# A selective scan whose products are shared by VectorE and GpSimd: which tiles GpSimd takes, when a pair of tiles is summed, and how much background work each step may start

## The chip, the cores and the metric

The kernel runs on one core of one Trainium2 chip. The metric is the device time of one execution in microseconds (us). TensorE (PE) multiplies matrices, VectorE (DVE), ScalarE (ACT) and GpSimd (POOL) compute on tiles, and SyncE (SP) issues nearly all transfers. All data are 32-bit floats.

## The reference, cut to what matters

Eight images of 64 x 64 positions and 96 channels go through two layers. The first is a state-space layer: a projection to 192 channels, a 3 x 3 convolution per channel, and then, along each of four directions over the 4,096 positions, a recurrence for every one of the 192 channels and 16 states.

```python
def step(h, inp):
    ul, dl, Bl, Cl = inp
    dA = jnp.exp(dl[..., None] * A)
    h = dA * h + (dl * ul)[..., None] * Bl[:, :, None, :]
    y = jnp.einsum('bkdn,bkn->bkd', h, Cl)
    return (h, y)
```

The four results are added, normalised, gated and projected back. The second layer doubles the resolution, applies a two-layer network with a quadratic activation and filters down again. Each layer's output is added to its input.

## The kernel before, in words

**The foreground: one tile per step.** A tile is 128 partitions (8 channels x 16 states) by 1,024 positions. 24 tiles (`NT`) cover the 192 channels of one chunk of 1,024 positions, four chunks (`NCH`) make a direction, and four directions (`k`, in the order 1, 0, 2, 3) make an image: 384 tiles an image, 3,072 in all. A loop takes one tile per step, so a step is the unit of everything below, and 96 steps (one direction) are called a quarter. A tile passes through these operations:

- `fetch` (L1001), six steps ahead: a transfer puts du (the product of dl and u) into `dub`, each channel's row repeated for its 16 states. Behind it, `product_b` (L1007) on GpSimd, three steps ahead: `bb = dub * br`.
- `decay` (L1013 and L1020), one step ahead: TensorE spreads dl over the states into the PSUM tile `pd`, and ScalarE takes the exponential in place. `pd` has two buffers, so the decay of tile p+1 has to wait until tile p-1 has left its buffer.
- `scan` (L1027) on VectorE: the recurrence. For most tiles its result overwrites `pd`. For a tile with the mark `by_pool` it goes to an SBUF tile `h`.
- `product_c` (L1033): `hc = h * cr`. VectorE does it straight after the scan. For a `by_pool` tile GpSimd does it in the next step, ahead of that step's `product_b`. These are called pooled tiles here.
- `hold` (L1037): the scan's last column is kept for the next chunk, by VectorE, or by ScalarE for a pooled tile.
- `sums` (L1056, and L1068, which adds what earlier directions left): TensorE adds the 16 states, for two tiles at a time, into `py`. Then ScalarE copies `py` out (L1089) and it is stored. `hc` has four buffers.

So an unpooled tile leaves its `pd` after scan, product and hold. A pooled tile leaves it right after the scan.

**The order.** Each engine works its instructions in the order in which the loop issues them. In one step this is: the pooled product of tile i-1, `product_b` of tile i+3, the decay of tile i+1, scan, product and hold of tile i, then background work, then (in every second step) the sums of a pair.

**The background.** All other work of both layers is written as generators that are advanced once per step: the preparation of the next chunk (px L924, pv L949, dl L965, u L968), convolution and gates of the next image (L515 to L581), normalisation of the last one (ty, pm, po, L637 to L706) and its second layer (L749 to L873). Each piece states an estimated cost per engine. `advance` adds an allowance per step to what is left for each engine, up to a limit, and takes off the cost of what it starts; a piece that does not fit waits for a later step:

```python
CAPS = dict(pe=(2.1, 2.9), act=(2.3, 3.0), dve=(1.5, 1.5), pool=(1.4, 2.7))
self.left = {e: min(self.left.get(e, 0.0) + c, most) for e, (c, most) in caps.items()}
self.left["pe"] -= taken
```

`taken` is 0.95 for a step with sums, and as much again where L1068 runs. Independent of this, a pace for the whole image decides how many pieces may be under way. Before the loop there is a preparation of about 140 us, and after the last step the second layer of the last image is run out with no allowance.

Of the kernel before, what the change touches and what calls it, by code (L numbers as in the profile page):

```python
# [25 lines left out]
NT = DI // 8  # L26
# [11 lines left out]
class Side:  # L38
# [6 lines left out]

    CAPS = dict(pe=(2.1, 2.9), act=(2.3, 3.0), dve=(1.5, 1.5), pool=(1.4, 2.7))

    def __init__(self, pool):
        self.pool = pool
# [79 lines left out]
def kernel(ctx: ExitStack, tc: tile.TileContext, a: dict, out: bass.AP):  # L132
# [78 lines left out]
    with tc.tile_pool(name="ps0", bufs=1, space=PSUM) as ps0, tc.tile_pool(name="setup", bufs=1) as c0p:  # L211
# [41 lines left out]
        for quarter in range(2):  # L253
            for n in (SIDE, 64):
                at = cols[n, quarter] = slice(c0, c0 + n)
# [96 lines left out]
    side = Side(pss)  # L352
# [625 lines left out]
    tiles = []  # L978
    for b in range(images):
        for k in (1, 0, 2, 3):  # L980
            order = range(NCH) if k < 2 else range(NCH - 1, -1, -1)
            for n, c in enumerate(order):
                got = {}
                for i in range(NT):
                    q, n8 = divmod(i, 8)
                    s, j = n8 % 2, n8 // 2
                    tiles.append(
                        dict(b=b, k=k, i0=c * T, first=n == 0, i=i, q=q, s=s, j=j, g=8 * q + 4 * s + j, got=got)
                    )

                    beside = b > 0 if k == 1 else k == 3 and b == images - 1
                    tiles[-1]["by_pool"] = i % (4 if beside else 3) == 2
    carry = pp.tile([128, NT], F32, tag="carry", name="carry", bufs=1)

    summed = set()
# [1 line left out]
    def fetch(t):  # L997
        assert t["got"]["ready"]
        t["dub"] = sp.tile([128, T], F32, tag="dub", name="dub", bufs=4)
        g = t["g"]  # L1000
        nc.sync.dma_start(  # L1001
            t["dub"], t["got"]["du"][None, 8 * g : 8 * g + 8, :].to_broadcast([NS, 8, T])
        )

    def product_b(t):
        t["bb"] = sp.tile([128, T], F32, tag="bb", name="bb", bufs=4)
        nc.gpsimd.tensor_tensor(t["bb"], t["dub"], t["got"]["br"], ALU.mult)  # L1007

    def decay(t):
        pd = t["pd"] = psd.tile([128, T], F32, tag="pd", name="pd")  # L1010
        for hf in range(2):
            rows = slice(64 * hf, 64 * hf + 64)
            nc.tensor.matmul(  # L1013
                pd[:, MB * hf : MB * hf + MB],
                sel_b[rows, 4 * t["s"] + t["j"]].rearrange("p n c -> p (n c)"),
                t["got"]["dl"][rows, t["q"], :],
                start=True,
                stop=True,
            )
        nc.scalar.activation(pd, pd, AF.Exp, scale=neg_a[:, t["k"], t["g"] : t["g"] + 1])  # L1020
# [10 lines left out]
    def product_c(t):  # L1031
        t["hc"] = sp.tile([128, T], F32, tag="hc", name="hc", bufs=4)
        (nc.gpsimd if t["by_pool"] else nc.vector).tensor_tensor(t["hc"], t["h"], t["got"]["cr"], ALU.mult)  # L1033
# [7 lines left out]
    def parts(t):  # L1041

        o = y_dram[t["b"]][t["k"] % 2]
        q = t["q"]
        return [o[64 * q : 64 * q + 64, t["i0"] + MB * hf : t["i0"] + MB * hf + MB] for hf in range(2)]

    def sums(two):

        t0 = two[0]
        if t0["j"] == 0:  # L1050
            t0["got"]["py"] = psy.tile([128, MB], F32, tag="py", name="py")
        py = t0["got"]["py"]
        for t in two:
            for hf in range(2):
                r0 = 64 * hf + 32 * t["s"]
                nc.tensor.matmul(  # L1056
                    py[r0 : r0 + 32],
                    sel_r[:, t["j"], :],
                    t["hc"][:, MB * hf : MB * hf + MB],
                    start=(t["j"] == 0),  # L1060
                    stop=(t["j"] == 3 and t["k"] == 0),
                    skip_group_check=True,
                )

        if t0["j"] == 3 and t0["k"]:

            add = d_diag[:, t0["q"], :] if t0["k"] == 1 else ident
            nc.tensor.matmul(py, add, t0["got"]["yp"], start=False, stop=True, skip_group_check=True)  # L1068
# [17 lines left out]
    def store(t):  # L1086
        yield dict(act=0.7)
        yq = sp.tile([128, MB], F32, tag="yq", name="yq", bufs=1)
        nc.scalar.copy(yq, t["got"]["py"])  # L1089
        yield {}  # L1090
        for hf, part in enumerate(parts(t)):
            nc.sync.dma_start(part, yq[64 * hf : 64 * hf + 64])
        if t["q"] == Q3 - 1:
            if t["k"] == 3:
                summed.add((t["b"], t["i0"] // T))
            elif t["k"] == 2 and t["i0"] == 0:
                summed.add((t["b"], "even"))
# [3 lines left out]
    with tc.manual_schedule():  # L1101
        side.queue, rest = front(0)
        side.drain()
        side.urgent = prepare(0, tiles[0]["k"], tiles[0]["i0"], tiles[0]["got"])
        side.drain()
        n = len(tiles)
        for i in range(FETCH):
            fetch(tiles[i])
            if i >= FETCH - LEAD:
                product_b(tiles[i - FETCH + LEAD])  # L1110
        decay(tiles[0])
        begin, *side.later = prepare(0, tiles[NT]["k"], tiles[NT]["i0"], tiles[NT]["got"])
        side.urgent.append(begin)
        total = 1
        for i in range(n + 4):
            t = tiles[i] if i < n else None
            at = i % (NT * NCH * K)
            if t and t["i"] == 0:
                b = t["b"]
                if at == 0:  # L1120
                    y_dram[b] = [dr.tile([DI, L], F32, tag=f"y{o}", name=f"y{o}") for o in range(2)]
                    side.begun, hasty = 0, sum(item[1] for item in rest) if b == 0 else 0
                    side.queue += rest
                    down, end = [], []
                    if b:
                        keep = {}
                        side.queue += tail(b - 1, keep)
                        up, down, end = mlp(b - 1, keep)
                        side.queue += up
                    if b + 1 < images:  # L1130
                        start, rest = front(b + 1)
                        side.queue += start[:2] + [i for two in zip(down, start[2:10]) for i in two] if b else start[:10]
                        side.queue += start[10:] + rest
                        rest = []
                    else:
                        side.queue += down
                    side.queue += end
                    total = sum(item[1] for item in side.queue)
                if b == images - 1 and at == NT * NCH * (K - 1):
                    keep = {}  # L1140
                    side.queue += tail(b, keep, pairs=False)
                    total = 0

            if i % NT == 20 and i + 4 + NT < n:
                nxt = tiles[i + 4 + NT]
                begin, *side.later = prepare(nxt["b"], nxt["k"], nxt["i0"], nxt["got"])
                side.urgent.append(begin)
            if i % NT == 0:
                side.urgent += side.later
                side.later = []  # L1150
            if t and t["i"] % 8 == 4:
                before(t)
            if i + FETCH < n:
                fetch(tiles[i + FETCH])
            if 0 < i <= n and tiles[i - 1]["by_pool"]:
                product_c(tiles[i - 1])
            if i + LEAD < n:
                product_b(tiles[i + LEAD])
            if i + 1 < n:
                decay(tiles[i + 1])  # L1160
            if t:
                scan(t)
                if not t["by_pool"]:
                    product_c(t)
                hold(t)
            ends = i % 2 == 1 and 3 <= i <= n + 2
            adds = ends and tiles[i - 2]["j"] == 3 and tiles[i - 2]["k"]
            side.advance(
                Side.CAPS,
                2 if not total or side.begun < max(hasty, total * at / 290) else 0,  # L1170
                0 if 7 <= i % NT <= 21 else 1,
                0.95 * (bool(ends) + bool(adds)),
            )
            if ends:
                sums(tiles[i - 3 : i - 1])
                if tiles[i - 2]["j"] == 3:
                    side.stores.append([g := store(tiles[i - 2]), next(g)])
        up, down, end = mlp(images - 1, keep)
        side.queue += up + down + end
        side.drain()  # L1180
# [89 lines left out]
```

## Time and profile before

| | |
|---|---|
| time, median of 3 runs | 11,521.71 us (11,514.94 to 11,524.55) |
| the profiled execution | 11,526.07 us, span 11,524.0 us |
| busy in the span | DVE 10,419.6 us, POOL 10,195.9 us, PE 9,523.4 us, ACT 5,877.0 us |
| mean granted TensorE clock | 0.913 |
| transfers | 2,401 MB, mean 208 GB/s |
| first scan starts, last sums start | 143.7 us, 11,241 us |

A scan takes VectorE about 2.3 us and a product 1.2 us; the same product takes GpSimd 2.36 us. The matmuls of one decay are four records in the trace and take about 1.1 us together. The profile's chain of what ended last holds only the run-out after the last scan, so the stretch that matters, the 3,072 steps, has to be read from the groups, the waits and the timeline. A wait that depends on several semaphores is named after the one that came last, so the engine named is not always the one that was late.

### The profile page before, as it was taken

The numbers are of one execution on the slowest core, as the hardware profiler recorded it, in microseconds if no ns is written. First come the engines' busy times: TensorE is split into PE (matmuls) and PEld (weight loads), VectorE is DVE, ScalarE is ACT, GpSimd is POOL, SyncE is SP. The second block draws the span as 40 slices with busy tenths as digits, with TensorE's granted clock in tenths as the row PEclk, the third lists the DMA queues.
The fourth block names the chain that finished last, engine by engine and source line by source line (L and its number), as shares of the span: only waits on it lengthen the run. The fifth ranks groups of instructions, "written<-read, shape, count | busy, mean of one in ns | idle before, by whom it ended". The sixth has DMA issues, their size and how long they took to land. (4 is left out here: it accounts for less than half of the span.)

```text
span 11524.0 us, 133552 instructions
## 1 busy us (share of the span) xinstructions
PE 9523.4 (83%) x42840; PEld 3036.7 (26%) x42840; DVE 10419.6 (90%) x8549; ACT 5877.0 (51%) x8210; POOL 10195.9 (88%) x4729
## 2 busy tenths in 40 slices
PE   7787768988789887888779897798977989788878
PEld 2121112322123222332223321232212322123225
DVE  5999999999999999999999999999999999899990
ACT  4455444556455454555545555454554546445443
POOL 4899998989989899999999998998999989899980
PEclk8898888999899998999889998899989999889987
DMA  6888898889988898898988889888898889988971
GB/s 150 205 196 221 201 217 202 209 217 233 221 201 212 214 229 217 207 215 216 235 204 215 213 210 240 201 213 212 218 234 205 214 212 232 218 200 211 230 189 47
DMA packets 1045088, 2401.01 MB, mean 208 GB/s; under 512 B 293948, under 2 KB 315708, under 8 KB 1044392
## 3 DMA queue, kind: packets, MB, share of 16 engines
q1 hardware_dynamic: 1040872, 2391.03, 84.3%
q8 instruction: 345, 5.65, 0.2%
q14 instruction: 351, 2.88, 0.1%
q10 hardware_dynamic: 3520, 1.46, 0.1%
HBM read 1929.05 MB, written 328.73 MB: 196 GB/s over the span
## 5 line engine op out<-in xcount | busy, mean ns | idle before, releaser
L1007 POOL TENSOR_TENSOR bb<-dub,br 128x1024 f32<-128x1024 f32 x3072 | 7174.9, 2358 | 357.9 <-DVE pd L1027 175.2
L1020 ACT ACTIVATE pd<-pd,neg_a 128x1024 f32<-128x1024 f32 x3072 | 3338.8, 1087 | 4952.4 <-PE pd L1013 4682.4
L1013 PE MATMUL pd<-dl,sel_b 64*128 64x512 f32 x12288 | 3833.8, 696 | 1781.3 <-DVE carry L1037 1556.1
L1027 DVE TENSOR_TENSOR_SCAN pd<-pd,carry,bb 128x1024 f32<-128x1024 f32 x1584 | 3722.4, 2350 | 328.0 <-ACT carry L1037 243.5
L1033 POOL TENSOR_TENSOR hc<-h,cr 128x1024 f32<-128x1024 f32 x960 | 2262.9, 2357 | 565.0 <-DVE h L1027 456.1
L1033 DVE TENSOR_TENSOR hc<-pd,cr 128x1024 f32<-128x1024 f32 x2112 | 2586.4, 1225 | 182.3 <-PE py L1056 43.5
L1013 PEld LDWEIGHTS pd<-dl,sel_b 64*128 64x128 f32 x12288 | 1053.2, 199 | 4243.7 <-issue 2837.3
L1056 PE MATMUL py<-hc,sel_r 128*32 128x512 f32 x12288 | 1839.2, 674 | 16.2 <-ACT yq L1089 15.5
L1027 DVE TENSOR_TENSOR_SCAN h<-pd,carry,bb 128x1024 f32<-128x1024 f32 x720 | 1684.3, 2339 | 51.6 <-ACT pd L1020 51.1
L1027 DVE TENSOR_TENSOR_SCAN pd<-pd,bb 128x1024 f32<-128x1024 f32 x528 | 1209.9, 2292 | 159.6 <-ACT carry L1037 129.8
L515 PE MATMUL pc<-pad,convr 96*128 96x512 f32 (+1 forms) x2304 | 867.9, 618 | 1.7 <-issue 1.7
L968 POOL TENSOR_TENSOR u<-dl,u 128x512 f32<-128x512 f32 x384 | 485.4, 1272 | 127.9 <-DMA br<-xd 127.8
L1027 DVE TENSOR_TENSOR_SCAN h<-pd,bb 128x1024 f32<-128x1024 f32 x240 | 547.4, 2281 | 17.3 <-ACT pd L1020 16.6
L1056 PEld LDWEIGHTS py<-hc,sel_r 128*32 128x32 f32 x12288 | 252.7, 113 | 1151.2 <-issue 838.8
L802 PEld LDWEIGHTS p<-w2q,mq 128*100 128x100 f32 x4800 | 454.5, 169 | 275.4 <-issue 212.4
L924 PE MATMUL px<-u,xp 64*64 64x512 f32 x1536 | 455.8, 650 | 78.6 <-DMA u<-u 78.6
L795 PE MATMUL ph<-xu,w 96*128 96x500 f32 x960 | 509.6, 635 | 10.9 <-ACT mq L796 6.1
L802 PE MATMUL p<-w2q,mq 128*100 128x96 f32 x4800 | 513.2, 259 | 2.7 <-ACT mq L796 2.7
L949 PE MATMUL pv<-xd,dt_w 64*64 64x512 f32 x1536 | 412.1, 629 | 9.4 <-ACT xd L934 9.2
L515 PEld LDWEIGHTS pc<-pad,convr 96*128 96x128 f32 (+1 forms) x2304 | 264.1, 163 | 570.2 <-issue 564.1
L796 ACT ACTIVATE mq<-ph,b 128x500 f32<-128x500 f32 x480 | 322.1, 678 | 73.2 <-PE ph L795 71.1
L1037 DVE COPY carry<-pd 128x1 f32<-128x1 f32 x2112 | 311.7, 148 | 0.0
(142 smaller groups left out, 6259.1 us busy)
## 6 DMA issues: line engine op xcount, KB each, us to landing
dub<-du SPq DMA_DIRECT2D x3072, 512.0 KB
u<-u SPq DMA_DIRECT2D x256, 384.0 KB
du<-u SPq DMA_DIRECT2D x768, 128.0 KB
y<-yq SPq DMA_DIRECT2D x768, 128.0 KB
br<-xd SPq DMA_DIRECT2D x256, 256.0 KB
cr<-xd SPq DMA_DIRECT2D x256, 256.0 KB
yp<-y SPq DMA_DIRECT2D x384, 128.0 KB
yp<-u SPq DMA_DIRECT2D x192, 128.0 KB
```

Of the source, the lines that this page charges most:

```text
L515: nc.tensor.matmul(t[rows].rearrange("p (i j) -> p i j", i=8), weights[:, cs], v["pad"][:, 8 * blk + kw : 8 * blk + kw + 8, kh : kh + H], ...
L795: nc.tensor.matmul(t[:, :px], w1[:, m, :], xu, start=True, stop=True)
L802: nc.tensor.matmul(t[:SIDE, C * i : C * i + C], sq[:, m, row], w2q[:, m, :], start=(m == 0), stop=(m == 2))
L924: nc.tensor.matmul(p[rows], xp[rows, k, q, :], v["u"][rows, q, :], start=(q == 0), stop=(q == 2), skip_group_check=True,)
L949: nc.tensor.matmul(t[rows], dt_w[rows, k, 64 * q : 64 * q + 64], v["xd"][rows], start=True, stop=True, skip_group_check=True,)
L968: nc.gpsimd.tensor_tensor(v["u"][:, q, :], got["dl"][:, q, :], v["u"][:, q, :], ALU.mult)
L1007: nc.gpsimd.tensor_tensor(t["bb"], t["dub"], t["got"]["br"], ALU.mult)
L1013: nc.tensor.matmul(pd[:, MB * hf : MB * hf + MB], sel_b[rows, 4 * t["s"] + t["j"]].rearrange("p n c -> p (n c)"), t["got"]["dl"][rows, t[" ...
L1020: nc.scalar.activation(pd, pd, AF.Exp, scale=neg_a[:, t["k"], t["g"] : t["g"] + 1])
L1027: nc.vector.tensor_tensor_scan(t["h"][:, ::step], pd[:, ::step], t["bb"][:, ::step], 0.0 if t["first"] else held, ALU.mult, ALU.add)
L1033: (nc.gpsimd if t["by_pool"] else nc.vector).tensor_tensor(t["hc"], t["h"], t["got"]["cr"], ALU.mult)
L1056: nc.tensor.matmul(py[r0 : r0 + 32], sel_r[:, t["j"], :], t["hc"][:, MB * hf : MB * hf + MB], start=(t["j"] == 0), stop=(t["j"] == 3 and t ...
```

## The change

- Outside of the stretches called `beside` (direction 1 from the second image on, and direction 3 of the last image), the pooled tiles of a chunk were 2, 5, 8, ..., 23 and are now 2, 4, 8, 10, 14, 16, 20, 22. Their number stays. In `beside` stretches they stay at 2, 6, 10, ...
- The sums of tiles (0, 1) were issued at the end of step 3, those of (2, 3) in step 5 and so on. They are now issued at the end of steps 2, 4, ...
- The allowance depends on the step: for TensorE 2.2 per step (2.5 in the first 48 steps of the program) instead of 2.1, with a limit of 2.6 instead of 2.9 in odd steps; for VectorE 1.4 in the step of a pooled tile and otherwise 0.7 (first direction of an image) or 0.3, instead of 1.5 everywhere.

```diff
-    CAPS = dict(pe=(2.1, 2.9), act=(2.3, 3.0), dve=(1.5, 1.5), pool=(1.4, 2.7))
+    @staticmethod
+    def caps_of(i, at, pooled):
+        if i < 2 * NT:
+            return dict(pe=(2.5, 2.9), act=(2.3, 3.0), dve=(1.5, 1.5), pool=(1.4, 2.7))
+        dve = 1.4 if pooled else 0.7 if at < 4 * NT else 0.3
+        return dict(pe=(2.2, 2.6 if i % 2 else 2.9), act=(2.3, 3.0), dve=(dve, 1.5), pool=(1.4, 2.7))
...
-                    tiles[-1]["by_pool"] = i % (4 if beside else 3) == 2
+                    tiles[-1]["by_pool"] = i % 4 == 2 if beside else i % 6 in (2, 4)
...
-            ends = i % 2 == 1 and 3 <= i <= n + 2
-            adds = ends and tiles[i - 2]["j"] == 3 and tiles[i - 2]["k"]
+            ends = i % 2 == 0 and 2 <= i <= n
+            adds = ends and tiles[i - 1]["j"] == 3 and tiles[i - 1]["k"]
             side.advance(
-                Side.CAPS,
+                Side.caps_of(i, at, i < n and t["by_pool"]),
                 2 if not total or side.begun < max(hasty, total * at / 290) else 0,
                 0 if 7 <= i % NT <= 21 else 1,
                 0.95 * (bool(ends) + bool(adds)),
             )
             if ends:
-                sums(tiles[i - 3 : i - 1])
-                if tiles[i - 2]["j"] == 3:
-                    side.stores.append([g := store(tiles[i - 2]), next(g)])
+                sums(tiles[i - 2 : i])
+                if tiles[i - 1]["j"] == 3:
+                    side.stores.append([g := store(tiles[i - 1]), next(g)])
```

## The prediction

> **What bounds the kernel.** I read the page first (busy shares), then the waits of VectorE, then the timeline around single idle times, then the four quarters of one image.
>
> ```profile
> PE 9523.4 (83%) x42840; PEld 3036.7 (26%) x42840; DVE 10419.6 (90%) x8549; ACT 5877.0 (51%) x8210; POOL 10195.9 (88%) x4729
> PEclk8898888999899998999889998899989999889987
> ```
>
> VectorE sets the pace. The steps lie between 143.7 and 11,241 us; outside of that VectorE has about 364 us of its 1,104 idle. Inside, it is idle for some 740 us, and that is all that a change of order can win. GpSimd is busy 10,196 of the same 11,097 us, so it would be the next bound, some 900 us lower.
>
> ```profile
> DVE pd L1027 <- ACT carry L1037: 373.3, 526, 4.9
> DVE pd L1027 <- ACT pd L1020: 78.5, 140, 1.9
> DVE h L1027 <- ACT pd L1020: 67.7, 22, 12.7
> DVE hc L1033 <- PE py L1056: 43.5, 31, 5.2
> DVE pd L1027 <- POOL bb L1007: 28.1, 23, 10.5
> ```
>
> Here (total, times, longest) scans wait for ScalarE. The name carry misleads: in the timeline such a scan starts 0.10 us after the exponential of its own tile. The last line says that GpSimd is hardly ever late.
>
> ```profile
> 4330.69 0.15 DVE L1037 COPY carry<-pd 128x1 f32<-128x1 f32 x1
> 4330.98 2.08 PE L1013 MATMUL pd<-dl,sel_b 64*128 64x512 f32 x4 [3.07 <-DVE carry L1037]
> 4332.99 1.93 PE L1056 MATMUL py<-hc,sel_r 128*32 128x512 f32 x8
> 4334.22 0.15 DVE L1037 COPY carry<-pd 128x1 f32<-128x1 f32 x1
> 4334.29 2.29 DVE L1027 TENSOR_TENSOR_SCAN h<-pd,bb 128x1024 f32<-128x1024 f32 x1
> 4334.86 1.55 PE L1068 MATMUL py<-yp,d_diag 128*128 128x512 f32 x2
> 4336.34 1.99 PE L1013 MATMUL pd<-dl,sel_b 64*128 64x512 f32 x8
> 4337.52 1.09 ACT L1020 ACTIVATE pd<-pd,neg_a 128x1024 f32<-128x1024 f32 x1 [3.33 <-PE pd L1013]
> 4338.70 2.30 DVE L1027 TENSOR_TENSOR_SCAN pd<-pd,bb 128x1024 f32<-128x1024 f32 x1 [2.13 <-ACT carry L1037]
> ```
>
> This is a pooled tile p (its scan at 4334.29 writes h). The hold of p-1 ends at 4334.37, and from there the decay of p+1 could run. VectorE has only the scan of p to do meanwhile, 2.3 us, while decay and exponential need 0.15 + 1.06 + 0.04 + 1.09 + 0.10 = 2.44. So a hole of 0.15 to 0.3 us follows a pooled tile even at best. Here TensorE is still at sums and their addition (until 4336.4), the decay is 2 us late, and the hole is 2.13.
>
> Going through VectorE's timeline scan by scan: idle time ahead of the 960 scans that follow a pooled tile is 405 us; ahead of the 2,112 others 151 us; ahead of other instructions 184 us. Of the 405, 245 us lie at 249 scans whose decay started over 0.3 us after it was free to. By the parity of the pooled tile: 384 odd ones have 117 us (0.30 each), 576 even ones 288 us (0.50 each). In the kernel before, sums come ahead of the decay of p+1 exactly when p is even.
>
> ```profile
> 4298.68:4675.70 377.02, 284.91 (x1254) 81.14 (x1250) 345.05 (x301) 167.17 (x225) 340.20 (x168) 0.86 0.86 211
> 4675.70:5002.20 326.50, 298.25 (x1563) 116.03 (x1564) 311.86 (x243) 188.33 (x270) 308.38 (x140) 0.96 0.87 213
> 5002.20:5349.40 347.20, 296.16 (x1392) 101.10 (x1394) 321.87 (x260) 177.23 (x255) 312.62 (x145) 0.94 0.89 213
> 5349.40:5684.50 335.10, 296.02 (x1152) 76.18 (x1144) 321.22 (x259) 200.20 (x278) 313.36 (x141) 0.95 0.89 228
> ```
>
> These are the four quarters of the fourth image (length, then PE, PEld, DVE, ACT, POOL, clock). The first is the slowest, has the lowest clock and the most VectorE idle time, 32 us. Over images two to eight, the 168 holes of first quarters hold 142 us, all at even tiles.
>
> **The change, part by part.**
>
> *Pooled tiles at even places, sums in even steps.* No operation is added or removed: 960 pooled tiles before and after, so VectorE and GpSimd have the same busy time. Counting in both built programs the TensorE work issued between the decays of p and p+1, at the timeline's durations (sums 1.06, two px or pv 1.06, ph 1.05, a convolution tap 0.87): VectorE leaves room for about 2.5 us of it. Before, 236 of 960 places hold over 2.6 us, together 93 us too much; after, 9 places and 1.7 us. So the late decays nearly vanish. Value: outside the first quarters the even tiles' holes are 0.353 us each over 392 tiles, those of the odd tiles, which already have the new arrangement, 0.292 over 361. I take 0.27 for all 760 (0.02 less, as late decays of the odd tiles go too): 205 us. For the 200 of the first quarters there is no odd row; I take 0.45: a place without background and at half clock shows 1.2, about a quarter are such, and the rest are near 0.2. That is 90 us. Sum 295 against 405: **-110 us**. Ends: 0.21 each (what odd tiles at full clock show) gives -203; 0.35 with 0.7 in the first quarters gives 0.
>
> *Where the sums go.* They now stand ahead of the decay of p+2. That decay is free when the scan of p ends and is needed one full unpooled step later, which leaves room for about 2.8 us between the decays of p+1 and p+2. By the same count, places over it grow from 11 us of excess to 62 (335 places, mean about 2.95). With background VectorE work in the same step counted, from 9.5 to 49. In the old odd tiles, which have this order, the scan of p+2 waits 52 us over 362 tiles, about 17 of it at transfers that the second layer waits for. I take the static growth as it is: **+46 us**; ends 0 and, at twice the static excess (the late places in front of p+1 measured about that), +118.
>
> *The lag of two instead of three.* Buffers of hc come free a step earlier: `hc <- PE py`, 43.5 us, goes to about 5: **-38 us**. The pair always ends in an unpooled tile, whose hc is done before the sums' turn. The pooled one of the pair is done by GpSimd 2.36 us after it starts. With pooled tiles two apart, GpSimd has three operations (7.07 us) between two scans that end 6.3 us apart, so it starts 0.8 us late and ends 3.1 us after the scan; the sums' turn comes 5.0 us after it. Cost nothing; if a preparation's u (1.27 us) slips in, still nothing; behind two ty (3.0 us) 1.1 us would be lost, but those belong to first quarters, where pooled tiles are four apart. bb stays ahead: it is ready 4 to 11 us before its scan in nearly all steps. Stores of y, two issues a time on SP's queue, move one step earlier together with the copy they wait for; dub transfers behind them have six steps. The yp loads get four steps instead of five, some 14 us. No other transfer moves.
>
> *VectorE's allowance.* By the stated costs the background asks for about 0.25 us a step, so a bucket of 1.5 stays nearly full even at 0.3 a step. Background instructions that stand behind a pooled scan, where they fill a hole, go from 302 to 365 of 1,167; pooled steps with any, from 256 to 283. 27 x 0.3: **-8 us**. The lag does not grow: the last dl of a chunk comes in place 7 to 9 of its 24 steps, as before.
>
> *TensorE's allowance.* Total work is the same; the mean rate of 2.2 moves it little. The limit 2.6 in odd steps allows two taps of 0.87 there and not three, which is in the count above. One place gets worse: in first quarters px waits about 6 us for its u, then sums and addition at half clock now stand ahead of a needed decay: +3.4 and -2.6 in two steps, +0.8 for each of seven images, **+6 us**. First steps and run-out: the first scans wait for transfers, and the TensorE work behind the last decay is 203 us in both: nothing.
>
> **The sum**: -110 + 46 - 38 - 8 + 6 = -104 us on the profiled 11,526 us, which is 4 us above the median. From 11,522 that is 11,418, rounded to **11,420 us**.
>
> **A rule against it.** The Trainium skill, "TensorE: Matmul & The Clock Gate", Part 1, says that an idle TensorE falls back to half clock after a window of about 3.4 us without work and needs a busy one to return. The change empties exactly the stretch ahead of the critical decay. The row first: outside first quarters 59 of 361 decays behind odd pooled tiles ran at half clock (about 2.08 us instead of 1.13), against 23 of 392 behind even ones, where sums keep the engine busy; a half-clock hole is 0.71 us, a full one 0.21. Taken to the letter, the stretch, at most 2.5 us idle, never cools the engine: all holes near 0.21, and the sum is -197. The trace shows half-clock decays after idle times of 2.5 to 3.1 us, so I keep the trace's 16%, which is in the 0.27.
>
> **Rivals.** (A) *The new place of the sums is free.* Late decays go and nothing is paid at p+2: -203 - 38 - 8 + 6, and some of the 151 us ahead of other scans, say 20 more: about 11,260 to 11,370, middle 11,320. For it: unpooled scans have 1 us of slack on average. Against: the old odd tiles' 52 us. (B) *The wait only moves by one step.* +118 instead of +46 and holes of 0.30: about 11,505. For it: summed over p+1, p+2 and the next tile, the old odd tiles idle no less than the even ones outside first quarters. Against: first quarters, where most is won. (C) *Slower, by the clock.* Each further half-clock hole costs 0.5 us; some 210 more than the 16% eat the sum. If 60% of holes ran cold, 390 x 0.5 = +195: about 11,615. For it: the 59 against 23. Against: outside first quarters the mean work in the emptied stretch is still 1.1 to 1.5 us. (D) *GpSimd becomes the bound*: in second quarters it is busy 308 of 326.5 us, so they can lose at most some 18 us an image; I expect 3. Not deciding. That the allowances bind at all is doubtful for VectorE; its part is only 8 us.
>
> **How the numbers follow.** Base 0.60 (its own range 11,370 to 11,475), A 0.20, B 0.12, C 0.08. Two runs of this kernel can tell about 0.2%, 23 us, from no change. Base and A are faster; B ends half within and half below; so faster 0.86, same 0.06, slower 0.08. The range reaches from A's middle to B's near end: 11,310 to 11,495.
>
> **What would show it.** Right: idle ahead of scans behind pooled tiles near 300 us, `hc <- PE py` near zero, first quarters 8 to 12 us shorter, busy times unchanged, more idle ahead of scans two behind a pooled tile. Wrong: a lower granted clock with holes of 1.1 us (C), that last idle time near 120 us (B) or unchanged (A), or idle time that the count does not see, such as GpSimd waiting for more transfers.

## The result, and the profile after

The changed kernel takes 11,548.2 us (median of 18 executions, 11,527.1 to 11,557.8), the kernel before, measured beside it, 11,529.8 us (18 executions, 11,513.6 to 11,553.6). The ratio is 1.0013, with a 95% interval of 1.0006 to 1.0020: a loss of about 0.1%, small but clear of the noise. The forecast was 11,420 us with a range of 11,310 to 11,495: not only the number is wrong, the sign is too. The profiled execution took 11,551.8 us with a span of 11,550.0, against 11,526.1 and 11,524.0. In all that follows the lines of the changed kernel's steps have numbers 9 higher than before (scan L1036, decay L1022, sums L1065, product L1042).

Busy times and granted clock (tenths, one digit per fortieth of the span) on the page of the changed kernel:

```profile
PE 9555.2 (83%) x42840; PEld 3021.8 (26%) x42840; DVE 10407.8 (90%) x8549; ACT 5881.4 (51%) x8210; POOL 10190.5 (88%) x4729
PEclk8898888999899998999889998899988999899988
```

VectorE's instructions are as many as before, and the mean clock is nearly the same (0.911 against 0.913). VectorE's idle time has moved. Its waits (total, times, longest, in us):

```profile
DVE h L1036 <- ACT pd L1029: 283.7, 223, 12.6
DVE pd L1036 <- ACT carry L1046: 251.2, 432, 4.7
DVE x L882 <- PE p L872: 218.1, 10, 182.8
DVE pd L1036 <- ACT pd L1029: 105.2, 203, 4.2
DVE e L547 <- ACT e L475: 64.1, 8, 21.4
DVE pd L1036 <- POOL bb L1016: 37.1, 26, 10.3
```

The row of scans behind a pooled tile (pd <- carry) fell from 373.3 to 251.2, and the product's wait for the sums (hc <- py, 43.5) is gone. But the scans of the pooled tiles themselves, the ones that write h, now wait 283.7 us where it was 67.7. The four quarters of the fourth image (length, then PE, PEld, DVE, ACT, POOL, clock):

```profile
4303.80:4672.20 368.40, 274.17 (x1240) 75.89 (x1240) 344.63 (x302) 165.42 (x220) 337.32 (x165) 0.88 0.87 213
4672.20:5011.30 339.10, 310.64 (x1578) 118.64 (x1578) 310.88 (x243) 190.73 (x274) 311.63 (x143) 0.95 0.85 208
5011.30:5351.70 340.40, 294.52 (x1402) 99.47 (x1402) 318.90 (x262) 177.31 (x256) 312.98 (x145) 0.94 0.89 219
5351.70:5692.00 340.30, 294.92 (x1136) 75.19 (x1132) 321.69 (x259) 200.80 (x278) 312.78 (x141) 0.94 0.88 224
```

First and third quarters became shorter (377.0 to 368.4 and 347.2 to 340.4), second and fourth longer (326.5 to 339.1 and 335.1 to 340.3). Over images two to eight the means are 376.6, 326.4, 346.1, 339.0 before and 369.8, 338.0, 342.4, 342.6 after, 4.7 us an image more.

Going through VectorE's timeline in the same way as before gives the whole account (idle us inside the steps):

| idle ahead of | before | after | difference |
|---|---|---|---|
| scans behind a pooled tile | 405.2 | 308.8 | -96 |
| scans of pooled tiles | 68.9 | 306.0 | +237 |
| other scans | 82.4 | 89.7 | +7 |
| products and all else | 183.7 | 77.3 | -106 |
| sum | 740.2 | 781.8 | +42 |

VectorE is busy 12 us less, so the steps take 30 us longer. The first scan starts 1.8 us earlier (141.9 against 143.7), and the last one ends 28 us later (11,267.9 against 11,239.9). One group won nearly what was hoped for (96 of 110), one won more (106, where 38 were hoped for), and the scans of the pooled tiles lost all of it.

This is what the loss looks like, in the timeline at a pooled tile at the start of a second quarter (start, duration, engine, line, operation; idle time and its end in brackets):

```profile
4672.45 2.08 PE L1022 MATMUL pd<-dl,sel_b 64*128 64x512 f32 x4 [3.72 <-DVE carry L1046]
4674.46 1.97 PE L933 MATMUL px<-u,xp 64*64 64x512 f32 x4
4675.69 0.15 DVE L1046 COPY carry<-pd 128x1 f32<-128x1 f32 x1
4675.76 2.30 DVE L1036 TENSOR_TENSOR_SCAN pd<-pd,bb 128x1024 f32<-128x1024 f32 x1
4676.36 1.93 PE L1065 MATMUL py<-hc,sel_r 128*32 128x512 f32 x8
4678.10 1.23 DVE L1042 TENSOR_TENSOR hc<-pd,cr 128x1024 f32<-128x1024 f32 x1
4678.23 1.23 PE L1077 MATMUL py<-yp,d_diag 128*128 128x512 f32 x2
4679.39 1.13 PE L1022 MATMUL pd<-dl,sel_b 64*128 64x512 f32 x4
4681.75 2.29 DVE L1036 TENSOR_TENSOR_SCAN h<-pd,bb 128x1024 f32<-128x1024 f32 x1 [2.37 <-ACT pd L1029]
4684.35 1.06 PE L1065 MATMUL py<-hc,sel_r 128*32 128x512 f32 x8
```

The buffer for the pooled tile's decay is free from 4675.84, but the decay starts 3.55 us later. TensorE had waited 3.72 us ahead of the decay of the tile before (4672.45); that decay runs at half clock (2.08 us instead of the 1.13 us at 4679.39), and so do px and the sums of the pair before: 1.93 us for what takes 1.06 us at 4684.35. The scan of the pooled tile waits 2.37 us.

### The profile page after: what moved, and what is told of

Its sections match the earlier page's. It is cut to its first block, busy times and chain, and to the rows that moved or that the text cites. A ratio compares the mean times of both kernels' runs of the same rounds, so it can differ in the third digit from the quotient of the medians.

```text
span 11550.0 us, 132188 instructions
## 1 busy us (share of the span) xinstructions
PE 9555.2 (83%) x42840; PEld 3021.8 (26%) x42840; DVE 10407.8 (90%) x8549; ACT 5881.4 (51%) x8210; POOL 10190.5 (88%) x4729
## 4 chain that ended last, share of the span: by engine, by line
DVE 32%; PE 30%; issue 13%; DMA 9%; POOL 9%; ACT 7%; SPq 1%; DVEq 0%; ACTq 0%; POOLq 0%
DVE pd L1036 22%; PE pd L1022 12%; POOL bb L1016 6%; DMA dub<-du 5%; PE py L1065 5%; ACT pd L1029 5%; PE pc L524 4%; DVE h L1036 4%; DVE hc L1042 3%; PE px L933 2%; PE ph L804 2%; DVE carry L1046 1%; PE p L811 1%; PE py L1077 1%; POOL hc L1042 1%
## 5 line engine op out<-in xcount | busy, mean ns | idle before, releaser
L1022 PE MATMUL pd<-dl,sel_b 64*128 64x512 f32 x12288 | 3805.4, 693 | 1743.9 <-DVE carry L1046 1653.0
L1036 DVE TENSOR_TENSOR_SCAN pd<-pd,carry,bb 128x1024 f32<-128x1024 f32 x1584 | 3721.7, 2350 | 241.5 <-ACT carry L1046 139.9
L1042 POOL TENSOR_TENSOR hc<-h,cr 128x1024 f32<-128x1024 f32 x960 | 2261.2, 2355 | 564.0 <-DVE h L1036 533.3
L1042 DVE TENSOR_TENSOR hc<-pd,cr 128x1024 f32<-128x1024 f32 x2112 | 2586.1, 1224 | 72.8
L1022 PEld LDWEIGHTS pd<-dl,sel_b 64*128 64x128 f32 x12288 | 1042.3, 198 | 4194.1 <-issue 3228.9
L1065 PE MATMUL py<-hc,sel_r 128*32 128x512 f32 x12288 | 1879.4, 687 | 40.4 <-POOL hc L1042 35.4
L1036 DVE TENSOR_TENSOR_SCAN h<-pd,carry,bb 128x1024 f32<-128x1024 f32 x720 | 1686.3, 2342 | 243.5 <-ACT pd L1029 222.9
L1036 DVE TENSOR_TENSOR_SCAN pd<-pd,bb 128x1024 f32<-128x1024 f32 x528 | 1209.9, 2291 | 157.1 <-ACT carry L1046 111.3
L1036 DVE TENSOR_TENSOR_SCAN h<-pd,bb 128x1024 f32<-128x1024 f32 x240 | 547.5, 2281 | 62.4 <-ACT pd L1029 60.7
L1065 PEld LDWEIGHTS py<-hc,sel_r 128*32 128x32 f32 x12288 | 254.6, 114 | 1216.6 <-issue 793.0
```

The source lines that it names most:

```text
L1022: nc.tensor.matmul(pd[:, MB * hf : MB * hf + MB], sel_b[rows, 4 * t["s"] + t["j"]].rearrange("p n c -> p (n c)"), t["got"]["dl"][rows, t[" ...
L1036: nc.vector.tensor_tensor_scan(t["h"][:, ::step], pd[:, ::step], t["bb"][:, ::step], 0.0 if t["first"] else held, ALU.mult, ALU.add)
L1065: nc.tensor.matmul(py[r0 : r0 + 32], sel_r[:, t["j"], :], t["hc"][:, MB * hf : MB * hf + MB], start=(t["j"] == 0), stop=(t["j"] == 3 and t ...
```

## The experiments

The theories that the expectations name: (1) the sums now stand ahead of a pooled tile's decay, and their place costs what was won; (2) the allowance by the kind of step costs it; (3) pooled tiles two apart are too fast for GpSimd or TensorE; (4) sums cost the same in any place; later (5), it is the clock: where TensorE has little to do it falls to half, and the sums, which now follow the emptied stretch, run at half clock just ahead of a decay that is waited for. A decay is counted as one at half clock when it takes over 1.6 us.

**The old allowance.** In the changed kernel, all three kinds of allowance go back to the old constant:

```diff
-                Side.caps_of(i, at, i < n and t["by_pool"]),
+                Side.CAPS,
```

> The changed kernel with the old allowance (2.1 and 1.5 in all steps). Theory 1, the place of the sums decides: idle time ahead of the scans of pooled tiles stays near the 306 us of the changed kernel, and the time stays within 20 us of it, 11,530 to 11,565 us. Theory 2, the new allowance spreads background work so that TensorE and ScalarE stall at the head of their queues: with the old one the time falls to 11,450 to 11,500 us.

Measured: 11,553.2 us (12 executions), ratio to before 1.0019 (1.0009 to 1.0030). Idle ahead of pooled tiles' scans is 265.6 us, behind them 323.4. Theory 2 falls: the two allowances differ by 5 us in medians, which can't be told from nothing. The allowance alone on the old order wasn't tried.

**The places alone.** In the kernel before, only the pooled places move; the sums stay in odd steps:

```diff
-                    tiles[-1]["by_pool"] = i % (4 if beside else 3) == 2
+                    tiles[-1]["by_pool"] = i % 4 == 2 if beside else i % 6 in (2, 4)
```

> Only the pooled places change (2, 4, 8, 10, ...); sums stay in odd steps, so they stand ahead of the decay that follows every pooled tile; old allowance. Theory 1: idle ahead of scans behind pooled tiles rises from 405 to some 480 us, idle ahead of the scans of pooled tiles stays under 80 us, time 11,570 to 11,620 us. Theory 3, two pooled tiles two apart are too fast a stretch for TensorE and GpSimd wherever the sums are: over 150 us ahead of the scans of pooled tiles, time over 11,640 us.

Measured: 11,566.5 us (8 executions), ratio 1.0036 (1.0022 to 1.0050). Now all sums stand ahead of the decay behind a pooled tile, and the row of waits that stands for it has grown from 373.3:

```profile
DVE pd L1027 <- ACT carry L1037: 464.3, 591, 4.9
```

By the timeline, idle time behind pooled tiles is 519.4 us, ahead of their own scans 60.0. Two apart is not too fast by itself: theory 3 falls. In medians the change is therefore made of +37 us (places), -13 (the sums' step and lag) and -5 (allowance), taken in this order; the second is hardly above the noise and the third is within it.

**Old places, sums postponed.** In the kernel before, sums that are due in the step ahead of a pooled tile wait one step more, so that they never stand ahead of the decay behind it:

```diff
+            if i % 2 == 1 and 3 <= i <= n + 2:
+                due.append(i)
+            ends = due and not (i + 1 < n and tiles[i + 1]["by_pool"])
+            e = due.pop(0) if ends else 0
...
-                sums(tiles[i - 3 : i - 1])
+                sums(tiles[e - 3 : e - 1])
```

> The kernel before with one rule more: sums that would be issued in the step ahead of a pooled tile's are issued one step later. So sums stand neither ahead of the decay behind a pooled tile nor, in stretches with every fourth tile pooled, ahead of the decay of a pooled tile. Theory 1: idle behind pooled tiles falls from 405 to some 310 us, ahead of pooled tiles it stays under 90, other scans gain under 40 us more idle: 11,440 to 11,480 us. Theory 4, sums cost the same in any place: 11,510 to 11,540 us.

Measured: 11,600.0 us (6 executions), ratio 1.0068 (1.0053 to 1.0083). A miss, on the far side. The part aimed at came: idle behind pooled tiles fell to 334.2 us, ahead of them to 43.1. But idle time grew ahead of the other scans (82.4 to 168.0) and ahead of products and all else (183.7 to 236.1). Of these last 52 us, some 39 come from a slower start of 574 more products, which is described under the lag of two below. The number of decays behind pooled tiles at half clock rose from 116 to 200 of 960. Theory 4 would have given 11,510 to 11,540 us, so it doesn't fit either; why the other scans lose 86 us was not followed.

**Thinner sums.** In the changed kernel, and below in the one before, half of the sums (the second and third of every four) are made over 128 of 512 columns; the rest of `y` is then incomplete:

```diff
+        w = MB if t0["j"] in (0, 3) else MB // 4
...
-                    py[r0 : r0 + 32],
+                    py[r0 : r0 + 32, :w],
                     sel_r[:, t["j"], :],
-                    t["hc"][:, MB * hf : MB * hf + MB],
+                    t["hc"][:, MB * hf : MB * hf + w],
```

> The changed kernel with half of its sums (those of the middle two of each four pairs) on 128 of 512 columns, so three quarters of their work are left out there. Theory 1: idle ahead of the scans of pooled tiles falls from 306 to between 130 and 200 us, time 11,380 to 11,450 us. If other work than the sums makes these decays late: idle over 250 us, time over 11,500 us.

Measured: 11,555.9 us (8 executions), ratio to before 1.0028 (1.0017 to 1.0039): work was taken off TensorE and nothing was won. Idle ahead of pooled tiles' scans fell only from 306.0 to 269.8 us, and behind them it rose from 308.8 to 355.5. On the page:

```profile
PE 9361.2 (81%) x42840; PEld 3129.3 (27%) x42840; DVE 10400.5 (90%) x8549; ACT 5886.5 (51%) x8210; POOL 10184.2 (88%) x4729
PEclk8788778989789988899889997898978989788877
```

The mean clock fell from 0.911 to 0.869, and decays at half clock rose from 354 to 628 of 3,072. Theory 1, taken as a matter of TensorE's amount of work, falls; theory 5 was formed here and is put to the test by the runs that follow. The same edit in the kernel before, run with the next group:

> The kernel before with half of its sums on 128 of 512 columns (the rest of them left out), as was done to the changed one. Theory 5: the clock falls to about 0.87 here too, what the shorter sums give is lost to half-clock decays, time 11,500 to 11,560 us. If sums in front of decays cost by their length at full clock: 11,420 to 11,470 us.

Measured: 11,593.8 us (3 executions), ratio 1.0046 (1.0026 to 1.0065), clock 0.875. It is slower with less work, and the expected 11,500 to 11,560 was too mild. In the changed kernel the loss is smaller (1.0028 against 1.0013), and the two intervals overlap.

**Useless work.** In a step without sums in which the background gave TensorE less than 1.0 us, a block of matmuls with zero weights is added into a sum that is open, which leaves its value. One block has the size of one step's sums, 1.06 us at full clock:

```diff
+            if not ends and py_open is not None and side.spent < 1.0:
+                warm(py_open)
             if ends:
                 sums(tiles[i - 2 : i])
+                py_open = tiles[i - 1]["got"]["py"] if tiles[i - 1]["j"] < 3 else None
```

> The changed kernel with useless matmuls (zero weights, added into the open py, 1.06 us a time) in steps without sums in which the background takes little of TensorE: the same result. Theory 5, sums at half clock are what makes the decays of pooled tiles late: the granted clock rises from 0.91 to over 0.94, idle ahead of the scans of pooled tiles falls from 289 to 100 to 170 us, and the time to 11,350 to 11,470 us although TensorE has more to do. If it is the amount of work on TensorE: later decays and over 11,550 us.

Measured: 11,435.3 us (5 executions), ratio to before 0.9908 (0.9892 to 0.9924).

```profile
PE 9679.5 (85%) x46848; PEld 3033.2 (27%) x46848; DVE 10397.9 (91%) x8549; ACT 5880.3 (51%) x8210; POOL 10196.3 (89%) x4730
PEclk8999999999999999999999999999999999999998
```

A block is 8 records, so (46,848 - 42,840) / 8 = 501 blocks were added, some 530 us of work at full clock; TensorE is busy only 124 us longer, since everything else became faster. The clock is 0.952, 176 decays run at half clock. Idle ahead of pooled tiles' scans fell from 306.0 to 203.4 us. The 289 of the expectation leaves out the first hundred steps; on that count it fell to 188, less far than the expected 100 to 170. The same in the kernel before:

> The same useless matmuls in the kernel before. Theory 5: granted clock over 0.94, idle behind pooled tiles falls from 405 to 280 to 340 us, time 11,400 to 11,490 us. If it is the amount of work: 11,540 us or more.

Measured: 11,445.3 us (6 executions), ratio 0.9916 (0.9899 to 0.9932), clock 0.949. Idle behind pooled tiles fell from 405.2 to 303.5 us. So the late decays of the kernel before, too, were in good part a matter of the clock.

**The mixed order.** First quarters as in the changed kernel, third quarters with its places and steps but the old allowance, second and fourth as before:

```diff
+                    tiles[-1]["new"] = k in (1, 2)
...
+            e = i - 1 if i % 2 == 0 else i - 2
+            ends = 1 <= e < n and tiles[e]["new"] == (i % 2 == 0)
...
+                Side.caps_of(i, at, i < n and t["by_pool"]) if at < 4 * NT else Side.CAPS,
```

> Per direction the arrangement that had the shortest quarter so far: first quarter as changed, second and fourth as before, third with the new places and steps but the old allowance. If what each arrangement does stays in its quarter: 370 + 326 + 337 + 335 us an image instead of 1,387, so 11,370 to 11,430 us. If the background moves from quarter to quarter: 11,500 to 11,550 us.

Measured: 11,510.4 us (13 executions), ratio 0.9976 (0.9967 to 0.9985). Quarter means of images two to eight: 369.1, 333.4, 341.1, 341.5. The first and third have what the changed kernel has. The second and fourth are 7 and 2.5 us longer than before, although their order is that of before: so what one quarter wins, the next partly loses. How (background work that moves over was expected) was not followed in the trace.

**More useless work, and useless work in the mixed order.** In the first, a second block is added in steps where the background gave TensorE less than 0.4 us; the second joins the two edits above.

```diff
                 warm(py_open)
+                if side.spent < 0.4:
+                    warm(py_open)
```

> The changed kernel with the useless matmuls (zero weights, added into an open sum, so that the result stays) once more: in the steps without sums where the background gave TensorE less than 1.0 us of work there is one block of 1.06 us as in the run before, and where it gave less than 0.4 us there are two. Theory 5 (the sums behind the emptied stretch run at half clock and then stand ahead of the decay of a pooled tile): half-clock sums get rarer still, idle time ahead of the scans of pooled tiles falls from the 203 us of one block towards 130 to 170, and the time is 11,390 to 11,430. If the second block only fills the room that the decay of the next tile needs, idle time behind pooled tiles rises by 30 to 100 us and the time is 11,440 to 11,520. If the clock is no matter any more: 11,435 as with one block.

Measured: 11,427.6 us (4 executions), ratio 0.9908 (0.9892 to 0.9925). The median lies within what theory 5 gave, but the ratio is that of one block, so the time doesn't show that the second block won anything. Idle ahead of pooled tiles' scans is 189.7 us and not 130 to 170. The clock is 0.961, and 122 decays run at half clock. Idle behind pooled tiles is 289.1 us as with one block, so the second block doesn't stand in the way. The row of waits that was 283.7 in the changed kernel (lines are 3 further on here):

```profile
DVE h L1039 <- ACT pd L1032: 162.8, 149, 13.2
```

> The mixed order (first and third quarters as in the changed kernel, third with the old allowance; second and fourth as before) with one useless block of 1.06 us in steps without sums where the background gave TensorE less than 1.0 us. If what the mixed order saves and what the clock saves are separate: 11,540 x 0.9976 x 0.991 = 11,410, range 11,395 to 11,430, ahead of both kernels with the useless blocks (11,435 and 11,445). If both remove the same idle time: 11,430 to 11,450.

Measured: 11,422.1 us (4 executions), ratio 0.9902 (0.9887 to 0.9916). The median lies in the range for two separate gains; by ratios these would give 0.9884, and the blocks alone 0.9908, so the run doesn't decide between the two. Its interval overlaps those of the other kernels with useless work, so it isn't shown to be the best of them; it has the lowest median, about 1% below both kernels without such work.

## Why the prediction was wrong

**"Pooled tiles at even places, sums in even steps" (-110): the size nearly came, for another reason.** The holes behind pooled tiles came to 308.8 us where 295 were forecast, so 96 us were won. 18.5 of these belong to TensorE's allowance below. The forecast put the gain down to work that no longer stands ahead of the decay, at full-clock durations for the most part. With the clock near full in both kernels (one block each) the order is worth 14 us there (289.5 against 303.5). That the number came close is luck.

**"The lag of two instead of three" (-38): right in kind, too small.** The wait for the sums went, but 106 us were won, nearly all ahead of products: their gaps over 0.05 us came to 142.6 us before and to none after. The forecast took the listed wait of 43.5 us alone. In VectorE's timeline before, a product of an even tile and then one of an odd tile:

```profile
5102.03 2.36 DVE L1027 TENSOR_TENSOR_SCAN pd<-pd,carry,bb 128x1024 f32<-128x1024 f32 x1 [0.29 <-ACT pd L1020]
5104.50 1.23 DVE L1033 TENSOR_TENSOR hc<-pd,cr 128x1024 f32<-128x1024 f32 x1
...
5106.90 2.35 DVE L1027 TENSOR_TENSOR_SCAN pd<-pd,carry,bb 128x1024 f32<-128x1024 f32 x1
5109.28 1.23 DVE L1033 TENSOR_TENSOR hc<-pd,cr 128x1024 f32<-128x1024 f32 x1
```

The first starts 0.10 us after its scan's end, the second 0.03. All 959 slow ones carry a wait for a semaphore of TensorE (for the buffer of `hc`) beside that for the scan, and none of the 1,153 others does. 917 of them start about 0.10 us behind the scan, 0.068 us later than the others: 62 us, of which no list of waits speaks. In the changed kernel no product carries such a wait, and all 2,112 start 0.03 to 0.04 us behind the scan.

**"Where the sums go" (+46): this is the step that failed.** The place was right, the cost was not: the forecast priced the sums at full clock. Place 26 (the 26th of the 96 steps of a first quarter, counted from 0) is treated with TensorE's allowance below. Outside it, idle time ahead of pooled tiles' scans rose from 32.7 to 234.3 us, by 202. Sorted by the clock of the sums that stand ahead of the pooled tile's decay (us):

| idle ahead of pooled tiles' scans, outside place 26 | before | after | one block | two blocks |
|---|---|---|---|---|
| behind sums at full clock (under 1.5 us) | 4.6 | 49.9 | 53.4 | 44.9 |
| behind sums at half clock (1.5 us and over) | 14.3 | 171.7 | 68.5 | 62.5 |
| no sums there | 13.8 | 12.6 | 12.8 | 13.2 |

Sums at full clock added 45 us: this is the count at full-clock durations, which had said 46. Sums at half clock added another 157, for which the forecast had nothing. They take 1.93 us instead of 1.06, and what follows them can begin cold. Keeping TensorE busy removes 103 us of this part and leaves the other as it was, so that the clock makes at least that much is shown; the 68 us that stay stand behind the half-clock sums that are left. The forecast's upper end of +118 took twice the static excess, from late places ahead of p+1 in the kernel before.

The change did not make much more time at half clock: within the steps it is 1,840 us before and 1,911 after, and 244 and 292 of the 1,536 sums run at half clock. It moved them. Ahead of a pooled tile's own decay stood 34 such sums before and 215 after; ahead of the decay behind a pooled tile 109 before and none after. Of the 215, 142 follow a decay that itself ran at half clock, and TensorE had waited 2.5 us (median) ahead of it.

**"A rule against it": weighed at the wrong instruction.** The Trainium skill, "TensorE: Matmul & The Clock Gate", Part 1, was held against the decay behind the pooled tile. There the trace's row held and the rule to the letter did not: 130 of 960 such decays run at half clock (14%; 16% were taken, against none by the rule). But the stretch's next instructions are the sums; emptied of them, it leaves them to meet the clock when it is down. Nor does the clock wait for an idle window. In the trace before, each stretch at half clock within the steps lasts a multiple of 3.41 us, so the clock changes on a grid of that width. It fell 290 times in the steps; in 280 of the 3.41 us stretches just ahead TensorE was busy for less than half of the time, against 35 of the 2,414 stretches after which it stayed at full clock (after the change: 302 of 330, and 29 of 2,361). So a stretch that is more than half empty is enough; the longest single wait in the 6.8 us ahead of a fall was 2.1 us (median). Rival C named the clock, but at the decay of p+1, where little changed; rival B named the right place (p+2), but priced it at 118 us without the clock, against 202 measured (and its terms give some 11,513 us, not 11,505).

**"TensorE's allowance" (+6 at one place of first quarters): right mechanism, too small.** The forecast said +3.4 and -2.6 us an image at the two steps; measured are +5.1 at place 26 (36.2 to 71.7 us over seven images) and -2.6 at the next (19.7 to 1.2). In the fourth image:

```profile
4397.55 1.97 PE L933 MATMUL px<-u,xp 64*64 64x512 f32 x2 [8.64 <-DMA u<-u]
4400.06 1.96 PE L933 MATMUL px<-u,xp 64*64 64x512 f32 x2 [0.55 <-DMA u<-u]
4401.96 1.93 PE L1065 MATMUL py<-hc,sel_r 128*32 128x512 f32 x8
4403.82 1.90 PE L1077 MATMUL py<-yp,d_diag 128*128 128x512 f32 x2
4405.65 1.13 PE L1022 MATMUL pd<-dl,sel_b 64*128 64x512 f32 x4
4408.02 2.35 DVE L1036 TENSOR_TENSOR_SCAN h<-pd,carry,bb 128x1024 f32<-128x1024 f32 x1 [10.44 <-ACT pd L1029]
```

After a long wait for a transfer px, sums and addition all run cold, one after the other, ahead of the decay. The useless blocks don't help there (69 us with one or two).

**VectorE's allowance (-8): not shown.** Both allowances together made 5 us in medians, within the noise.

**The sum.** -96 + 202 + 7 - 106 + 35 = +42 us of idle time, less 12 of busy time. With the clock near full in both kernels, 10 us are left of the change (11,435 against 11,445), which can't be told from nothing. Behind pooled tiles the idle time is then 289.5 against 303.5, ahead of them 203.4 against 84.8, other scans 102.2 against 84.7, all else 76.5 against 183.6. VectorE is busy 23 us less, which outweighs the 15 us more of idle time. So most of the 96 us won was not the order but the cold engine in it: the kernel before saves it as well once TensorE is kept busy. Of the 119 us that remain ahead of pooled tiles, 52 stand behind sums at full clock (53.4 against 1.1 in the kernel before with blocks): these are the order alone. Most of the rest stands behind sums that are still at half clock; why the blocks don't reach these was not followed.

## What to carry to other kernels

When matrix work is moved out of a stretch, cost what comes behind the stretch at half clock as well as what stands in it, and look in the trace for the same instruction at both durations before a count at one duration is believed. Here a stretch of 3.41 us in which TensorE was busy for less than half of the time nearly always cost the full clock. If a kernel's bound waits for short matmuls and TensorE has room, try a little useless work in the thin steps before rearranging the order: here it won 0.8% to 0.9% where the rearrangement won nothing. Count idle time ahead of every instruction of the bounding engine from its timeline, not only listed waits.

## What was not expected of the hardware

- Less TensorE work won nothing in either order: in the changed one 194 us less busy time (9,361.2 against 9,555.2) came with a clock of 0.869 instead of 0.911 and a time 0.28% above the kernel before, where the changed kernel is at 0.13% and the intervals overlap. In the old order it lost 0.46%. More work made both faster: one block (501 in all) gave a clock of 0.952 and a time 0.92% below the kernel before; up to two blocks (844 in all) gave 0.961 and the same time.
- A wait for a TensorE semaphore beside that for the scan goes with 0.068 us more between scan and product (0.10 instead of 0.034, 917 times), which the list of waits doesn't show. No product without it starts so. In the order with postponed sums 1,533 products start so, and idle time ahead of products is 215 us.
- GpSimd working beside it didn't slow VectorE's product: 1.22 to 1.23 us throughout, with GpSimd busy 88% of the span. Some small operations do wait for it: of the 15 executions of L445 (96 x 1) behind the first scan of the kernel before, 7 find no GpSimd instruction running and take 0.22 us; the other 8 take 1.1 to 2.3 us and end within 0.02 us of GpSimd's instruction.
